# Mamba's first chunk: diagonals on GpSimd, both images' norms ahead of it, four PSUM buffers for its step sizes, the first state's products on VectorE

## The chip, the cores and the metric

The kernel runs on one core of a Trainium2 chip. The metric is the device time of one execution in microseconds (us). The core has five engines with a queue each: TensorE (PE in the profile), VectorE (DVE), ScalarE (ACT), GpSimd (POOL), and SyncE (SP), which here only issues DMAs. A queue is worked off in its order; an instruction that waits holds back all that stand behind it.

## The reference

The network has four layers on an input of 2 images, 256 channels and 32x32 positions. Only layer 0 is touched by the change. Cut to what it computes:

```python
x = x + layer0(group_norm(x))                 # groups of 8 channels, per image
# layer0: two Mamba blocks, the second on flipped channels
xs, res = split(u @ in_w + in_b)              # u: tokens x 256; xs, res: tokens x 512
xs = silu(causal_conv(xs, conv_w, 4 taps) + conv_b)
dt, B, C = split(xs @ xproj_w)                # 16, 16 and 16 columns
delta = softplus(dt @ dt_w + dt_b)            # the step sizes, tokens x 512
h[t] = exp(delta[t] * A) * h[t-1] + delta[t] * B[t] * xs[t]    # 16 states a channel
y[t] = sum over states of h[t] * C[t] + xs[t] * D
out = (y * silu(res)) @ out_w + out_b
u = u + layernorm(out)
```

Layers 1 to 3 (a 7x7 attention by convolution, linear attention with a mixture of experts, softmax attention with another) follow layer 0 and are the same in both kernels.

## The kernel before

All 2048 tokens of both images lie in `x`, channels on the partitions: two chunks of 128 channels by 1024 positions for each image. A Mamba block is worked off in four chunks of 512 tokens, the first two of image 0 and the last two of image 1; with two blocks there are eight units (`units` in `layer0`). A unit has three parts.

- `front` computes the inputs of the scan for one chunk: the projection `m_in` (L300) to `pre`, the convolution over four positions, `xd` (the small projection, L342) and its transposed third `ct`, then the step sizes: four matmuls `m_dt` (L370), one for each 128 of the 512 channels, and from each, softplus by |z|, Exp, Ln and corrections. `e` is the Exp, `ln` the logarithm, `delta` the step size, `du` the step size times `xs`. The very first `front` runs `alone=True`, ahead of any scan: its softplus and products are VectorE's and go by single channel blocks `dc`, and two of its four channel blocks are convolved by VectorE (L314, L319); the other two, like all of the later chunks, by TensorE with diagonal matrices (`taps`, L327).
- `scan` runs over 16 states `n`. For each, GpSimd forms two products `h = du * b` of 128x1024 (L450), where `b` is a row of B spread by DMA over the partitions; ScalarE forms the decay `da` in PSUM (L457); VectorE runs four scans of 512 tokens (L461). TensorE transposes the result into a PSUM bank `ht` (L429) and VectorE adds it, weighted by C, to `ya` (L438); for states 0 and 10 ScalarE writes it (L436). There are six buffers for `h`, that is three states.
- `back` applies the gate, the skip term (by the diagonal `skip` on TensorE, L496), the output projection and the layer norm.

Unit by unit, the scan of one unit, the front of the next and the back of the last are emitted interleaved: `paced` gives out steps of the others in 63 slots, one for each scan instruction. `load` fetches a block's weights and makes `taps`, 16 diagonals of 128x128, each the identity times a column of weights (L257); `load_rest` fetches the gate and output weights and makes the four `skip` diagonals (L277). For block 2 these are emitted in the steps of unit 3 and in those of unit 4.

This emitted order is a priority and not yet the queues' order. A planner goes over the whole program with estimated durations and gives each engine, when it takes it to be free, the first instruction in emitted order that it takes to be ready; buffers of a pool are handed out at the same time. So instructions can stand far ahead of their place in the source: the diagonals of block 2 ran at 348 to 367 us, in the third unit.

`GroupNorm.image(b)` normalises an image: `bn_stats` (L207) and `bn_aggr` (L208) for each channel's mean and variance, a matmul with a block matrix for the mean over the group (`gn_ps`, L210), the deviation (L215 to L217), a second matmul (L219), the square root on ScalarE (L146), and the normalisation in place (L225), four instructions of 128x512 for each image.

PSUM in this layer has eight banks: two for `mm` (all matmuls of front and back), three for `ht` (the transposes of the scan), three for `da`.

Of the kernel before, what the change touches and what calls it, by code (L numbers as in the profile page):

```python
# [19 lines left out]
P = 128  # L20
# [7 lines left out]
TC = 512  # L28
# [152 lines left out]
class GroupNorm:  # L181
# [18 lines left out]
    def image(self, b):  # L200
# [3 lines left out]
        for cc in range(NCC):  # L204
# [3 lines left out]
            nc.vector.bn_aggr(out=mv[:, cc, :], in_=st.rearrange("p h s -> p (h s)"))  # L208
        ps = self.psum.tile([P, TC], F32, tag="mm", name=f"gn_ps{b}")
        nc.tensor.matmul(ps[:, :n], lhsT=self.grp, rhs=mv[:, :, 0], start=True, stop=True)  # L210
# [6 lines left out]
        nc.vector.tensor_add(d, d, mv[:, :, 1])  # L217
        ps = self.psum.tile([P, TC], F32, tag="mm", name=f"gn_ps2{b}")
        nc.tensor.matmul(ps[:, :n], lhsT=self.grp, rhs=d, start=True, stop=True)  # L219
# [10 lines left out]
class Mamba:  # L230
# [14 lines left out]
    def load(self):  # L245
        net, nc, m, wpool = self.net, self.net.nc, self.m, self.wpool
        in_w, out_w, xproj_w, dt_w = self.weights
        self.in_sb = wpool.tile([P, NCC, DI], F32, tag="in_w", name=f"{m}_in_sb")
        nc.sync.dma_start(self.in_sb, in_w[:, :, :DI])
        self.xp_sb = wpool.tile([P, NDC, XD], F32, tag="xproj_w", name=f"{m}_xp_sb")  # L250
        nc.sync.dma_start(self.xp_sb, xproj_w)
        self.dt_sb = wpool.tile([RANK, DI], F32, tag="dt_w", name=f"{m}_dt_sb")
        nc.sync.dma_start(self.dt_sb, dt_w)

        self.taps = wpool.tile([P, NDC * 4, P], F32, tag="taps", name=f"{m}_taps")
        for i in range(NDC * 4):
            nc.vector.tensor_scalar_mul(  # L257
                self.taps[:, i, :], net.ident, net.col(f"{m}_conv_w", i)
            )
        self.aneg = wpool.tile([P, NDC * NS], F32, tag="aneg", name=f"{m}_aneg", bufs=2)  # L260
        nc.scalar.activation(self.aneg, net.col(f"{m}_A_log", 0, NDC * NS), AF.Exp)
        nc.vector.tensor_scalar_mul(self.aneg, self.aneg, -1.0)
        self.state = wpool.tile([P, NS, NDC], F32, tag="state", name=f"{m}_state", bufs=2)

    def load_rest(self):
# [10 lines left out]
        for dc in range(NDC):  # L276
            nc.vector.tensor_scalar_mul(self.skip[:, dc, :], net.ident, net.col(f"{m}_D", dc))  # L277
        yield
# [5 lines left out]
    def front(self, j, alone=False):  # L284
# [83 lines left out]
        for dc in range(NDC):  # L368
            ps = self.ps_mm.tile([P, TC], F32, tag="mm", name=f"{m}_dt_{j}_{dc}")
            nc.tensor.matmul(  # L370
# [33 lines left out]

    def scan(self, j, before, between):

# [37 lines left out]
        for n in range(NS):  # L444
# [3 lines left out]
            for g in range(NDC // G):  # L448
                h = scanp.tile(half, F32, tag="h", name=f"{m}_h_{j}_{n}_{g}", bufs=6)
                nc.gpsimd.tensor_mul(  # L450
                    h, du[:, g * G : (g + 1) * G, :], b.unsqueeze(1).to_broadcast(half)
# [112 lines left out]
def layer0(net, x, x_dram, m1, m2, load_image, taps, conv_dram, lg):  # L564
# [5 lines left out]
    with (  # L570
# [14 lines left out]
        ]  # L585
        norm = GroupNorm(net, wpool, ps_mm, x)
        blocks[0].load()
        load_image()
        for _ in blocks[0].load_rest():
# [4 lines left out]
        norm.image(0)  # L594
        units = [(m, j) for m in blocks for j in range(NCH)]
        for _ in units[0][0].front(0, alone=True):
            pass
        norm.image(1)
        before, done = iter(()), []
        aside = taps.make(ps_mm, conv_dram)  # L600
        for u, (m, j) in enumerate(units):
            steps = [(b, Mamba.GATED, 0, 35) for b in done]
            fronts = []
            for a, k in units[u + 1 : u + 2]:
                if k == 0:
                    a.load()
                fronts.append(a.front(k))
            rest = m.load_rest() if u and j == 0 else iter(())
# [7 lines left out]
            else:  # L616
# [17 lines left out]
                steps += [(taps.convolve(0, pair, acc), 56, 3, 63)]  # L634
            before = m.scan(j, before, paced(63, steps))
            done = [m.back(j)]
# [1059 lines left out]
```

## Time and profile before

| | us |
|---|---|
| three runs: lowest, median, highest | 2225.58, 2238.22, 2242.52 |
| the profiled execution | 2231.08 |
| its span, first to last instruction | 2229.4 |
| first scan instruction starts (L461) | 56.7 |
| last scan instruction starts | 1045.8 |

| engine | busy us | share of the span | instructions |
|---|---|---|---|
| TensorE, matmuls | 1917.7 | 86% | 8072 |
| VectorE | 1413.0 | 63% | 2180 |
| ScalarE | 1009.8 | 45% | 1686 |
| GpSimd | 1006.7 | 45% | 688 |

The shares are means over stages with different limits. The Mamba layer takes from the start to about 1046 us, the other layers the rest. The mean granted clock of TensorE was 0.91 of full speed.

In a timeline, each line gives start and duration in us, the engine, the source line, the operation, the tile written, an arrow, the tiles read, shapes, and how many instructions were merged; in brackets stands the time that the engine had been idle and what ended it. The duration of a merged line is from its first start to its last end.

### The profile page before, as it was taken

The numbers are of one execution on the slowest core, as the hardware profiler recorded it, in microseconds if no ns is written. First come the engines' busy times: TensorE is split into PE (matmuls) and PEld (weight loads), VectorE is DVE, ScalarE is ACT, GpSimd is POOL, SyncE is SP. The second block draws the span as 40 slices with busy tenths as digits, with TensorE's granted clock in tenths as the row PEclk, the third lists the DMA queues.
The fourth block names the chain that finished last, engine by engine and source line by source line (L and its number), as shares of the span: only waits on it lengthen the run. The fifth ranks groups of instructions, "written<-read, shape, count | busy, mean of one in ns | idle before, by whom it ended". The sixth has DMA issues, their size and how long they took to land.

```text
span 2229.4 us, 24288 instructions
## 1 busy us (share of the span) xinstructions
PE 1917.7 (86%) x8072; PEld 1207.2 (54%) x8072; DVE 1413.0 (63%) x2180; ACT 1009.8 (45%) x1686; POOL 1006.7 (45%) x688
## 2 busy tenths in 40 slices
PE   4789888897989889788999899859999699769995
PEld 1455555655555555454656556536665367546663
DVE  5999999999999999898104565642222533532223
ACT  4586766767777767644113544312221232212121
POOL 1687684968688786964025410013332000033330
PEclk8869988798989989799999999969999799879997
DMA  2111120211212111310030100038987200079996
GB/s 104 38 60 47 39 66 28 62 34 48 61 47 59 38 48 34 84 42 15 18 49 1 48 15 10 19 146 309 309 311 264 80 10 10 19 249 314 316 310 257
DMA packets 90022, 223.94 MB, mean 100 GB/s; under 512 B 35003, under 2 KB 51264, under 8 KB 79268
## 3 DMA queue, kind: packets, MB, share of 16 engines
q1 hardware_dynamic: 81620, 202.77, 27.5%
q0 software_dynamic: 7728, 19.15, 3.0%
q8 instruction: 67, 1.10, 0.2%
q10 hardware_dynamic: 544, 0.40, 0.1%
q14 instruction: 63, 0.52, 0.1%
HBM read 204.88 MB, written 19.37 MB: 101 GB/s over the span
## 4 chain that ended last, share of the span: by engine, by line
PE 32%; DVE 22%; issue 20%; POOL 13%; ACT 8%; DMA 4%; POOLq 0%; SPq 0%; DVEq 0%; ACTq 0%
DVE m_h L461 11%; DVE m_ya L438 6%; POOL x L1465 3%; PE acc L746 3%; POOL l_yd L1524 3%; POOL m_h L450 3%; PE m_ht L429 3%; PE early_acc L746 3%; PE av L1248 3%; DMA l_yd<-y,target 2%; PE sc L1222 2%; PE h L1083 2%; ACT m_da L457 2%; PE m_xd_ps L342 2%; PE w L1092 1%
## 5 line engine op out<-in xcount | busy, mean ns | idle before, releaser
L450 POOL TENSOR_TENSOR m_h<-m_du,m_b 128x1024 f32<-128x1024 f32 x256 | 602.2, 2375 | 241.0 <-PE m_ht L429 95.1
L429 PE MATMUL m_ht<-ident,m_h 128*128 128x128 f32 x2048 | 365.7, 308 | 135.8 <-DVE m_ya L438 83.8
L457 ACT ACTIVATE m_da<-m_delta,m_aneg 128x512 f32<-128x512 f32 x512 | 349.2, 690 | 224.1 <-DVE m_h L461 223.3
L429 PEld LDWEIGHTS m_ht<-ident,m_h 128*128 128x128 f32 x2048 | 265.1, 156 | 328.5 <-DVE m_ya L438 112.4
L1465 POOL DMA_INDIRECT x<-l_zd,source x82 | 83.5, 1018 | 599.9 <-DMA we<-in_l_experts_dram 223.5
L438 DVE SCALAR_TENSOR_TENSOR m_ya<-m_ht,m_ct,m_ya 128x512 f32<-128x512 f32 x448 | 318.7, 731 | 21.2 <-PE m_ht L429 20.9
L461 DVE TENSOR_TENSOR_SCAN m_h<-m_da,m_state,m_h 128x512 f32<-128x512 f32 x256 | 318.3, 1268 | 13.2 <-POOL m_h L450 8.0
L461 DVE TENSOR_TENSOR_SCAN m_h<-m_da,m_h 128x512 f32<-128x512 f32 x256 | 302.8, 1208 | 14.7 <-ACT m_da L457 11.5
L1493 PE MATMUL h<-we,xts 128*128 128x512 f32 x632 | 289.8, 602 | 2.5 <-DVE xts L1483 2.5
L1500 DVE TENSOR_TENSOR hid<-hid,h 128x512 f32<-128x512 f32 x79 | 54.3, 688 | 285.7 <-PE h L1493 281.8
L1493 PEld LDWEIGHTS h<-we,xts 128*128 128x128 f32 x632 | 115.8, 193 | 119.9 <-issue 116.4
L1511 ACT COPY hts<-ht 128x512 f32<-128x512 f32 x79 | 46.3, 586 | 276.6 <-PE ht L1507 276.6
L1518 PE MATMUL o<-we,hts 128*128 128x256 f32 x632 | 149.8, 380 | 2.2 <-DVE y L1523 1.5
L1524 POOL DMA_INDIRECT l_yd<-y,target x79 | 80.2, 1015 | 139.8 <-DVE y L1523 135.0
L1518 PEld LDWEIGHTS o<-we,hts 128*128 128x128 f32 x632 | 114.1, 190 | 16.6 <-issue 3.4
L327 PE MATMUL m_conv<-m_pre,m_taps 128*128 128x512 f32 x240 | 115.1, 603 | 6.5 <-ACT m_gate L487 5.6
L746 PE MATMUL early_acc<-x,early 128*98 128x448 f32 (+21 forms) x308 | 97.4, 448 | 0.0
L746 PE MATMUL acc<-x,pair 128*98 128x416 f32 (+21 forms) x308 | 94.2, 454 | 0.0
L1499 ACT ACTIVATE hid<-h 128x512 f32<-128x512 f32 x79 | 47.2, 597 | 87.9 <-PE h L1493 87.9
L1523 DVE COPY y<-o 128x256 f32<-128x256 f32 x79 | 33.6, 425 | 73.2 <-PE o L1518 73.2
L483 PE MATMUL m_g<-x,m_gate_sb 128*128 128x512 f32 x128 | 68.0, 641 | 2.1 <-ACT m_gate L487 1.3
L746 PEld LDWEIGHTS acc<-x,pair 128*98 128x98 f32 x308 | 47.9, 168 | 40.3 <-issue 34.8
(320 smaller groups left out, 2985.1 us busy)
## 6 DMA issues: line engine op xcount, KB each, us to landing
we<-in_l_experts_dram SPq DMA_DIRECT2D x82, 1536.0 KB
m_b<-m_bd SPq DMA_DIRECT2D x128, 256.0 KB
l_yl<-l_yd SPq DMA_DIRECT2D x16, 512.0 KB
w<-in_l_w_dram SPq DMA_DIRECT2D x21, 256.0 KB
l_zd<-l_z SPq DMA_DIRECT2D x8, 512.0 KB
early<-taps SPq DMA_DIRECT2D x7, 343.0 KB
pair<-taps SPq DMA_DIRECT2D x7, 343.0 KB
taps<-taps_sb SPq DMA_DIRECT2D x21, 98.0 KB
```

What stands on the lines that cost most here:

```text
L327: nc.tensor.matmul(ps, lhsT=self.taps[:, dc * 4 + k, :], rhs=pre[:, dc, k : k + TC], start=(k == 0), stop=(k == 3),)
L429: nc.tensor.transpose(ps[:, dc * P : (dc + 1) * P], hs[dc // G][:, dc % G, i * P : (i + 1) * P], net.ident,)
L438: nc.vector.scalar_tensor_tensor(ya[:, i, :], ps, c, ya[:, i, :], ALU.mult, ALU.add)
L450: nc.gpsimd.tensor_mul(h, du[:, g * G : (g + 1) * G, :], b.unsqueeze(1).to_broadcast(half))
L457: nc.scalar.activation(da, delta[:, dc, :], AF.Exp, scale=self.aneg[:, i : i + 1])
L461: nc.vector.tensor_tensor_scan(h, da, h, 0.0 if first else state[:, n, dc : dc + 1], ALU.mult, ALU.add)
L483: nc.tensor.matmul(ps, lhsT=self.gate_sb[:, kc, dc * P : (dc + 1) * P], rhs=xt[:, kc, tok], start=(kc == 0), stop=(kc == NCC - 1),)
L746: nc.tensor.matmul(a[:, lo - 16 * k : hi - 16 * k, co : co + n], lhsT=lhsT, rhs=self.x[:, kc, b, lo - r0 : hi - r0, ci : ci + n], start=(u ...
L1465: nc.gpsimd.indirect_dma_start(out=x, out_offset=None, in_=zd[:, :], in_offset=bass.IndirectOffsetOnAxis(ap=source[:, g : g + 1], axis=0), ...
L1493: nc.tensor.matmul(ps, lhsT=xt[:, kc * P : (kc + 1) * P], rhs=w12[:, s, kc, :], start=(kc == 0), stop=(kc == NCC - 1),)
L1518: nc.tensor.matmul(ps[:, :C], lhsT=ht[:, mc * P : (mc + 1) * P], rhs=w[:, 8 + mc, :], start=(mc == 0), stop=(mc == NHC - 1),)
L1524: nc.gpsimd.indirect_dma_start(out=yd[g], out_offset=bass.IndirectOffsetOnAxis(ap=target[:, g : g + 1], axis=0), in_=y, in_offset=None, bo ...
```

## The change

Four things change in layer 0.

- The 16 diagonals `taps` and the four `skip` of both blocks are made by GpSimd. The 16 are now a generator, `diagonals`: for block 1 it is run through after `load`, for block 2 it is handed out over the first eight slots of unit 3's steps.
- `norm.image(1)` is emitted right behind `norm.image(0)`, ahead of the first front, and both take their PSUM banks from the pool of the transposes, `ht`.
- In the first front (`alone`), the step-size matmuls of channel blocks 1 to 3 take their banks from `ht`, too, so that with one of `mm` four are in use.
- In the first unit, the products of state 0 are formed by VectorE.

```diff
@@ GroupNorm.image
-        ps = self.psum.tile([P, TC], F32, tag="mm", name=f"gn_ps{b}")
+        ps = self.psum.tile([P, TC], F32, tag="ht", name=f"gn_ps{b}")
...
-        ps = self.psum.tile([P, TC], F32, tag="mm", name=f"gn_ps2{b}")
+        ps = self.psum.tile([P, TC], F32, tag="ht", name=f"gn_ps2{b}")
@@ Mamba.load
         self.taps = wpool.tile([P, NDC * 4, P], F32, tag="taps", name=f"{m}_taps")
-        for i in range(NDC * 4):
-            nc.vector.tensor_scalar_mul(
-                self.taps[:, i, :], net.ident, net.col(f"{m}_conv_w", i)
-            )
...
+    def diagonals(self):
+
+        for i in range(NDC * 4):
+            self.net.nc.gpsimd.tensor_scalar_mul(
+                self.taps[:, i, :], self.net.ident, self.net.col(f"{self.m}_conv_w", i)
+            )
+            yield
@@ Mamba.load_rest
         for dc in range(NDC):
-            nc.vector.tensor_scalar_mul(self.skip[:, dc, :], net.ident, net.col(f"{m}_D", dc))
+            nc.gpsimd.tensor_scalar_mul(self.skip[:, dc, :], net.ident, net.col(f"{m}_D", dc))
@@ Mamba.front
-            ps = self.ps_mm.tile([P, TC], F32, tag="mm", name=f"{m}_dt_{j}_{dc}")
+            pool, tag = (self.ps_ht, "ht") if alone and dc else (self.ps_mm, "mm")
+            ps = pool.tile([P, TC], F32, tag=tag, name=f"{m}_dt_{j}_{dc}")
@@ Mamba.scan
-    def scan(self, j, before, between):
+    def scan(self, j, before, between, start=False):
...
-                nc.gpsimd.tensor_mul(
+                (nc.vector if start and n == 0 else nc.gpsimd).tensor_mul(
                     h, du[:, g * G : (g + 1) * G, :], b.unsqueeze(1).to_broadcast(half)
                 )
@@ layer0
-        norm = GroupNorm(net, wpool, ps_mm, x)
+        norm = GroupNorm(net, wpool, ps_ht, x)
         blocks[0].load()
+        for _ in blocks[0].diagonals():
+            pass
         load_image()
...
         norm.image(0)
         units = [(m, j) for m in blocks for j in range(NCH)]
+        norm.image(1)
         for _ in units[0][0].front(0, alone=True):
             pass
-        norm.image(1)
...
                 if k == 0:
                     a.load()
+                    steps.append((a.diagonals(), NDC * 4, 0, 8))
...
-            before = m.scan(j, before, paced(63, steps))
+            before = m.scan(j, before, paced(63, steps), u == 0)
```

## The prediction

> **What bounds the kernel now.** I first read the page's rows of busy tenths, to see which engine is full when. Each digit is one fortieth of the span, 55.7 us.
>
> ```profile
> PE   4789888897989889788999899859999699769995
> DVE  5999999999999999898104565642222533532223
> ```
>
> From slice 2 to slice 19, the Mamba layer, VectorE (DVE) stands at 9. Next the windows of that layer, with the sum of each engine's busy time:
>
> ```profile
> core 0: us, PE busy (x) PEld busy (x) DVE busy (x) ACT busy (x) POOL busy (x), PEclk, DMA share, GB/s
> 57.00:1046.00 989.00, 841.06 (x3883) 537.36 (x3883) 938.46 (x1081) 684.49 (x1105) 757.87 (x397) 0.88 0.17 48
> ```
>
> VectorE is busy 938 of 989 us (95%), TensorE 85%, GpSimd (POOL) 77%, ScalarE 69%. So from the first scan to the end of the layer VectorE is the bound, and an instruction taken off it there shortens the run by nearly its length. What follows 1046 us starts when the layer ends and is not touched. Ahead of 57 us no engine is full: there a chain decides. Its start, in the timeline of VectorE (start us, duration us, engine, line, operation; in brackets the idle time before):
>
> ```profile
> 8.31 3.19 DVE L257 TENSOR_SCALAR m_taps<-ident,cols_sb 128x128 f32<-128x128 f32 x16
> 11.42 0.87 DVE L277 TENSOR_SCALAR m_skip<-ident,cols_sb 128x128 f32<-128x128 f32 x4
> 12.20 0.15 DVE L212 COPY gn_gm<-gn_ps 128x2 f32<-128x2 f32 x1
> 15.52 1.91 DVE L225 TENSOR_SCALAR x<-x,gn_gm,gn_rs 128x512 f32<-128x512 f32 x4
> 22.80 0.55 DVE L314 TENSOR_SCALAR m_xs<-m_pre,cols_sb 128x512 f32<-128x512 f32 x1 [5.37 <-ACT m_pre L304]
> ```
>
> Image 0's group means are out of TensorE at 9.1 us (two L210 matmuls, 8.54 to 9.10), but VectorE builds 20 diagonals until 12.20 before it copies them. The first projection (L300) starts at 16.12, on the normalised image. VectorE is idle 5.37 us before 22.80. Then the step sizes, in the timelines of TensorE and ScalarE:
>
> ```profile
> 39.70 1.12 PE L370 MATMUL m_dt<-m_xd,m_dt_sb 16*128 16x512 f32 x2 [0.77 <-DVE m_delta L377]
> 42.71 2.07 PE L370 MATMUL m_dt<-m_xd,m_dt_sb 16*128 16x512 f32 x2 [1.89 <-DVE m_delta L377]
> 38.88 1.28 ACT L383 ACT_TABLE_LOAD   x1
> 43.02 1.28 ACT L386 ACT_TABLE_LOAD   x1
> 46.85 1.28 ACT L383 ACT_TABLE_LOAD   x1
> 48.79 1.28 ACT L386 ACT_TABLE_LOAD   x1
> ```
>
> With two PSUM buffers the third and fourth step-size matmuls wait for VectorE to empty a bank, so ScalarE goes Exp, Ln, Exp, Ln, with four table loads where two would do. The first scans, on VectorE:
>
> ```profile
> 54.01 2.71 DVE L399 TENSOR_TENSOR m_delta<-m_delta,m_ln 128x512 f32<-128x512 f32 x1
> 56.71 1.21 DVE L461 TENSOR_TENSOR_SCAN m_h<-m_da,m_h 128x512 f32<-128x512 f32 x1
> 59.63 1.31 DVE L217 TENSOR_TENSOR gn_d<-gn_d,gn_mv 128x2 f32<-128x2 f32 x1
> 64.58 8.73 DVE L225 TENSOR_SCALAR x<-x,gn_gm,gn_rs 128x512 f32<-128x512 f32 x4
> 73.23 4.55 DVE L461 TENSOR_TENSOR_SCAN m_h<-m_da,m_h 128x512 f32<-128x512 f32 x4
> ```
>
> Image 1's normalisation lies between the scans, at 2.2 us an instruction where image 0's took 0.54, while GpSimd runs seven products (L450) end to end. Last, the second Mamba block's diagonals, also in VectorE's queue:
>
> ```profile
> 348.13 4.95 DVE L257 TENSOR_SCALAR m_taps<-ident,cols_sb 128x128 f32<-128x128 f32 x8
> 361.98 0.46 DVE L257 TENSOR_SCALAR m_taps<-ident,cols_sb 128x128 f32<-128x128 f32 x2
> 363.61 3.43 DVE L257 TENSOR_SCALAR m_taps<-ident,cols_sb 128x128 f32<-128x128 f32 x6
> 629.64 2.78 DVE L277 TENSOR_SCALAR m_skip<-ident,cols_sb 128x128 f32<-128x128 f32 x3
> ```
>
> **What the Trainium skill says.** "SBUF — State Buffer", section "SBUF: two separate sides": VectorE and GpSimd share one pair of SBUF ports under an exclusive lock, which a VectorE instruction needs if it has two SBUF inputs or runs in a 2-port mode. The trace agrees: L225 0.54 against 2.24 us, L399 0.68 against 2.71, each beside L450 on GpSimd (2.36 us); the scan, with one input in PSUM, stays at 1.21. "ScalarE activation tables", section "What a function is on this engine": a switch of set is one load of 1283 ns; here 1.28.
>
> **The change, part by part.** Durations are of the profiled execution, 2231.1 us with a span of 2229.4.
>
> *Diagonals of block 1 to GpSimd.* Takes 3.19 + 0.78 us from VectorE ahead of 12.20. The copy of the means can then start at 9.2. From there to the first L225 took 3.3 us before (12.20 to 15.52), with image 1's statistics between the small steps; I keep that, since by the bytes moved image 1 lands at about 9.3 and 10.5 us. L225 at 12.5, L300 at 13.1: **-3.0 us** (-1.5 if a statistic stands in the queue before its data are there, -4 if none stands between). GpSimd is idle from 2.3 us on. A tensor_scalar on it is not in the trace. Nearest rows: affine_select on 128x128, 0.28 to 0.40 us; the product, 2.36 us for 1024 elements of two inputs. "GPSIMD Engine Reference", section "Elementwise — side-by-side cycle accounting", puts short bodies at 1.03 cycles an element. So 0.2 to 0.5 us, I take 0.35: begun with the columns at 5.5, the sixteen end at 11.1 and the skip's four at 12.5; the first conv matmul comes at 22.3 (25.3 - 3). Cost nothing. GpSimd's next work is the carry copy at 23, so nothing else queues behind them.
>
> *Image 1's normalisation before the first chunk.* Its 4 x 0.48 us of L225 and some 1 us of small steps fall behind image 0's, 14.4 to about 18, into the idle before L314 (19.8 after the shift): nothing, with 1.8 us of margin; without that cover it costs up to 3 us. TensorE gets four tiny matmuls (0.59 us a pair) and ScalarE one square root earlier, ahead of the first pre-activation at 17. Out of the scan stage go L225's 8.7, L217's 1.3, 0.6 of small steps, and on ScalarE two table loads.
>
> *Four buffers for the step sizes.* Count from the end of m_xd (36.53 before, 33.5 after). Before, the first Ln ended 8.5 us later; now four Abs go first (1.65 + 4 x 0.61 = 4.1), load (5.4), four Exp (7.75), load (9.05), Ln at 9.75: the first Ln is 1.3 us *later*. But by then VectorE has done all that hangs on Abs and Exp (4 x 0.70 + 4 x 0.95 = 6.6 us). The three banks from the transposes' pool are empty at about 8 us, long before the first transposes: nothing.
>
> *First state's products on VectorE.* Two tensor_mul of 128x1024, not in the trace on VectorE; 0.69 us for 512 elements and 0.53 of it streaming give 1.14 a piece back to back: +2.3. They spare the 5.46 us wait for GpSimd's first product, which VectorE's own tensor_tensors kept from the port (50.72 to 56.18).
>
> *Sum for the first chunk*, VectorE from the first Ln to the end of the fifth scan: 12 x 0.605 (softplus and du) + 2.3 + 5 x 1.13 + 0.5 left over + one port block of 2.1 (as L399's) = 17.8, so at 9.75 + 17.8 = 27.6 after m_xd. Before, that scan ended at 64.4 and VectorE was free for the next at 73.2, 36.7 after m_xd. Gain **-9.1** (-11.2 with no block, -5 with three). Next is VectorE again: GpSimd needs 4.7 us a state for two products, VectorE 7 to 8.
>
> *Block 2's diagonals.* VectorE loses 4.86 + 0.37 + 3.35 us of L257 and 2.71 + 0.71 of L277: 12.0 us (intervals to the next start). TensorE waited 5.4 us at 354.39 for VectorE, so they are on the path; I take **-10.5**, and -7 to -12 as bounds. GpSimd gets 20 x 0.35 = 7 us in a stage where it idles 12.6 us at 351.8 to 364.5 and three products lie ready ahead of the scans: nothing. The diagonals issue no DMA.
>
> Total -22.6: 2231.1 becomes 2208.5. The median, 2238.2, lies 7 us above the profiled run, and the four known runs (2225.6, 2231.1, 2238.2, 2242.5) have a mean of 2234.4. Taken from that mean: **2212 us**.
>
> **Rivals.** (a) *The port lock.* GpSimd starts the second state's products as soon as du is half done and alternates with VectorE's remaining tensor_tensors at 2.2 us each, as it did with L225. For: exactly that at 64.58. Against: VectorE's five back-to-back tensor_tensors at 51.48 to 53.89 kept GpSimd out. With five blocks the first chunk gains nothing: 2234.4 - 13.5 = 2221. (b) *VectorE's freed time becomes waiting* for TensorE, at 85% and a granted clock of 0.88: half of the second block's and the scan stage's gain lost, 2234.4 - 12 = 2222. For: TensorE's share. Against: the 5.4 us it waited. (c) *Nothing*: the order in the queues is planned over the whole layer, and another order gives the gain back: 2234. (d) *Slower: a GpSimd tensor_scalar costs d, far over 0.35 us.* Place: the conv diagonals of the first chunk (the twelfth, for its third channel block, is needed at 25.7, begun at 5.5: late by 12d - 20.2) and block 2's sixteen ahead of products (three states ahead, 23 us: late by 16d - 23). Price 28d - 43.2; it eats 22.6 at d = 2.35, and from d = 3.2 the run is slower by 1%, 2257. Against: affine_select at 0.28 to 0.40.
>
> **How the numbers follow.** Forecast 0.60, (a) 0.17, (b) 0.11, (c) 0.07, (d) 0.05. The forecast's own bounds are the sums of the ends, -13.5 to -27.2, and the runs of before spread by 8 us either way. One per cent, about what a measurement of this kernel can tell from no change, is 22.4 us: 2215.8. The forecast lies below it about 8 times in 10, (a) and (b) 2 in 10: 0.54 faster, 0.39 within, 0.07 slower. Range: 2198 (-27 and 9 for the runs) to 2229, which takes in (a) and (b).
>
> **What would show it.** Right: L212 near 9.3 us, L300 near 13; one Exp and one Ln load between Abs and the scans; no L225 after 20 us and all near 0.5; first scan near 49 to 51, the sixth near 61; L257 and L277 on GpSimd near 0.35 us; no such row on VectorE after 60. Wrong: tensor_tensors of 2 us or more on VectorE after the first du; diagonals over 1.7 us (12d = 20.2); more idle on VectorE between 80 and 1000 us, ended by TensorE or GpSimd.

## The result, and the profile after

| | before | after |
|---|---|---|
| median (range) of 4 executions, us | 2234.53 (2225.58 to 2242.52) | 2210.97 (2210.15 to 2212.91) |
| profiled execution, its span | 2231.08, 2229.4 | 2212.91, 2211.0 |
| first scan instruction ends | 57.9 | 55.0 |
| 16th (after four of the 16 states) | 91.6 | 78.6 |
| 64th (end of the first unit) | 178.4 | 164.7 |
| 192nd (end of the third unit) | 432.2 | 416.6 |
| 512th, the last | 1047.1 | 1031.8 |

After over before is 0.9897, 95% interval 0.9855 to 0.9938: faster by 1.0%. The forecast was 2212 us.

The lines of layer 0 moved down by three to six (before to after): L257 to L263 (taps), L277 to L280 (skip), L300 to L303 (`m_in`), L370 to L374 (`m_dt`), L377 to L381, L383 to L387 (Exp), L386 to L390 (Ln), L391 to L395, L395 to L399, L397 to L401, L399 to L403, L401 to L405 (du), L429 to L434 (transposes into `ht`), L438 to L443, L450 to L455 (products), L457 to L462 (decay), L461 to L466 (scan).

The rows of busy tenths, and the window from the first scan to the end of the layer, after:

```profile
PE   6888898897978888789999899859999699769995
DVE  6999998999999999897114666542222533532223
```

```profile
core 0: us, PE busy (x) PEld busy (x) DVE busy (x) ACT busy (x) POOL busy (x), PEclk, DMA share, GB/s
57.00:1028.00 971.00, 829.10 (x3859) 527.56 (x3858) 912.98 (x1050) 676.72 (x1096) 763.94 (x415) 0.89 0.17 49
```

The window stops 3.8 us short of the last scan's end, that of before only 1.1 us. Taken to that end in both, VectorE has 22.8 us less to do (939.56 to 916.78) in a stretch that is 15.3 us shorter; it is still the fullest engine, 94% against 95%. Where it happened, in VectorE's timeline after, from the start to the third unit:

```profile
8.65 0.16 DVE L212 COPY gn_gm<-gn_ps 128x2 f32<-128x2 f32 x1 [0.74 <-PE gn_ps L210]
...
10.90 1.29 DVE L207 BATCH_NORM_STATS2 gn_st<-x 128x6 f32<-128x512 f32 x2 [1.40 <-DMA x<-in_x_dram]
...
12.35 2.02 DVE L225 TENSOR_SCALAR x<-x,gn_gm,gn_rs 128x512 f32<-128x512 f32 x4
...
21.59 1.91 DVE L225 TENSOR_SCALAR x<-x,gn_gm,gn_rs 128x512 f32<-128x512 f32 x4
...
52.07 1.22 DVE L455 TENSOR_TENSOR m_h<-m_du,m_b 128x1024 f32<-128x1024 f32 x1
53.20 0.68 DVE L405 TENSOR_TENSOR m_du<-m_delta,m_xs 128x512 f32<-128x512 f32 x1
53.80 1.22 DVE L466 TENSOR_TENSOR_SCAN m_h<-m_da,m_h 128x512 f32<-128x512 f32 x1
54.94 2.40 DVE L455 TENSOR_TENSOR m_h<-m_du,m_b 128x1024 f32<-128x1024 f32 x1
57.26 7.90 DVE L466 TENSOR_TENSOR_SCAN m_h<-m_da,m_h 128x512 f32<-128x512 f32 x7
...
344.91 2.34 DVE L466 TENSOR_TENSOR_SCAN m_h<-m_da,m_h 128x512 f32<-128x512 f32 x2 [4.83 <-POOL m_h L455]
```

The means are copied at 8.65 instead of 12.20. Then VectorE waits 1.40 us for image 1's data with image 0's normalisation behind it in its queue. Image 1's normalisation now takes 1.91 us at 21.59, not 8.73 us between scans. One product (2.40 against 1.22) stood against GpSimd's products at the port. The last line is new: at 344.91 VectorE waits 4.83 us for a product of GpSimd's. The step sizes, on TensorE and on ScalarE:

```profile
34.69 3.69 PE L374 MATMUL m_dt<-m_xd,m_dt_sb 16*128 16x512 f32 x8
```

```profile
36.61 1.28 ACT L387 ACT_TABLE_LOAD   x1
...
41.84 1.28 ACT L390 ACT_TABLE_LOAD   x1
45.71 1.28 ACT L462 ACT_TABLE_LOAD   x1
```

The four matmuls (the profile lists two records for each) run without a pause; there is one load for Exp and one for Ln; the third, at 45.71, is the decay's. Last, GpSimd's timeline after, with the diagonals:

```profile
5.21 0.61 POOL L263 TENSOR_SCALAR m_taps<-ident,cols_sb 128x128 f32<-128x128 f32 x1 [3.37 <-DMA cols_sb<-in_cols_dram]
...
6.18 9.49 POOL L263 TENSOR_SCALAR m_taps<-ident,cols_sb 128x128 f32<-128x128 f32 x15
15.65 2.33 POOL L280 TENSOR_SCALAR m_skip<-ident,cols_sb 128x128 f32<-128x128 f32 x4
...
53.90 19.53 POOL L455 TENSOR_TENSOR m_h<-m_du,m_b 128x1024 f32<-128x1024 f32 x8
...
333.26 9.29 POOL L263 TENSOR_SCALAR m_taps<-ident,cols_sb 128x128 f32<-128x128 f32 x16
342.51 4.67 POOL L455 TENSOR_TENSOR m_h<-m_du,m_b 128x1024 f32<-128x1024 f32 x2
```

A diagonal takes 9.29 / 16 = 0.58 us on GpSimd, and block 2's sixteen stand in one piece ahead of products.

So the gain came early: -13.7 us by the end of the first unit, and only 1.6 us more from there to the last scan (-15.3), where the prediction had 10.5. The span is shorter by 18.3; the last 3 us lie behind the layer (1182.3 to 1179.2 us), in code that is the same. Of the other profiled kernels below, all with that code, none took over 1180.4 there, so that the 1182.3 belongs to this one execution of before and those 3 us are not the change's. From the 16th scan to the last, VectorE waited 48.5 us before (20.3 of it for TensorE, 11.1 for GpSimd) and 57.5 after (18.8 and 18.9). What the experiments had to find is where block 2's 10.5 us went.

### The profile page after: what moved, and what is told of

The parts are those of the page before. It is cut to its first block, busy times and chain, and to the rows that moved or that the text cites. A ratio compares the mean times of both kernels' runs of the same rounds, so it can differ in the third digit from the quotient of the medians.

```text
span 2211.0 us, 24284 instructions
## 1 busy us (share of the span) xinstructions
PE 1915.3 (87%) x8072; PEld 1201.8 (54%) x8072; DVE 1391.4 (63%) x2142; ACT 1003.4 (45%) x1682; POOL 1026.0 (46%) x726
## 3 DMA queue, kind: packets, MB, share of 16 engines
q1 hardware_dynamic: 81620, 202.77, 27.6%
## 4 chain that ended last, share of the span: by engine, by line
PE 32%; DVE 22%; issue 20%; POOL 11%; ACT 10%; DMA 4%; POOLq 0%; SPq 0%; DVEq 0%; ACTq 0%
DVE m_h L466 11%; DVE m_ya L443 6%; POOL x L1473 3%; PE acc L754 3%; POOL l_yd L1532 3%; PE m_ht L434 3%; PE early_acc L754 3%; PE av L1256 3%; ACT m_da L462 2%; DMA l_yd<-y,target 2%; PE sc L1230 2%; PE h L1091 2%; POOL m_h L455 2%; PE m_xd_ps L345 1%; PE w L1100 1%
## 5 line engine op out<-in xcount | busy, mean ns | idle before, releaser
L455 POOL TENSOR_TENSOR m_h<-m_du,m_b 128x1024 f32<-128x1024 f32 x254 | 594.3, 2365 | 196.3 <-PE m_ht L434 96.1
L434 PE MATMUL m_ht<-ident,m_h 128*128 128x128 f32 x2048 | 362.8, 306 | 117.7 <-DVE m_ya L443 81.9
L462 ACT ACTIVATE m_da<-m_delta,m_aneg 128x512 f32<-128x512 f32 x512 | 349.4, 690 | 220.4 <-DVE m_h L466 219.8
L434 PEld LDWEIGHTS m_ht<-ident,m_h 128*128 128x128 f32 x2048 | 260.5, 155 | 316.3 <-DVE m_ya L443 111.3
L443 DVE SCALAR_TENSOR_TENSOR m_ya<-m_ht,m_ct,m_ya 128x512 f32<-128x512 f32 x448 | 320.2, 733 | 18.8 <-PE m_ht L434 17.2
L466 DVE TENSOR_TENSOR_SCAN m_h<-m_da,m_state,m_h 128x512 f32<-128x512 f32 x256 | 318.5, 1270 | 13.5 <-POOL m_h L455 8.5
L466 DVE TENSOR_TENSOR_SCAN m_h<-m_da,m_h 128x512 f32<-128x512 f32 x256 | 303.1, 1209 | 23.6 <-ACT m_da L462 13.2
L303 PE MATMUL m_in<-x,m_in_sb 128*128 128x512 f32 x128 | 68.8, 663 | 10.2 <-ACT m_pre L307 6.9
```

The costliest lines, as they stand in the source:

```text
L303: nc.tensor.matmul(ps, lhsT=self.in_sb[:, kc, mc * P : (mc + 1) * P], rhs=self.xt[:, kc, tok], start=(kc == 0), stop=(kc == NCC - 1),)
L434: nc.tensor.transpose(ps[:, dc * P : (dc + 1) * P], hs[dc // G][:, dc % G, i * P : (i + 1) * P], net.ident,)
L443: nc.vector.scalar_tensor_tensor(ya[:, i, :], ps, c, ya[:, i, :], ALU.mult, ALU.add)
L455: (nc.vector if start and n == 0 else nc.gpsimd).tensor_mul(h, du[:, g * G : (g + 1) * G, :], b.unsqueeze(1).to_broadcast(half))
L462: nc.scalar.activation(da, delta[:, dc, :], AF.Exp, scale=self.aneg[:, i : i + 1])
L466: nc.vector.tensor_tensor_scan(h, da, h, 0.0 if first else state[:, n, dc : dc + 1], ALU.mult, ALU.add)
```

## Experiments

Two readings of the missing gain stood against each other. **The lump:** VectorE's time is worth its length, and it was lost because GpSimd's sixteen diagonals, at 0.58 us and in one piece, hold back a product that VectorE then waits for. **Waiting for TensorE**, the prediction's rival (b): VectorE's freed time is mostly not to be had, whatever GpSimd does. The single parts were then run alone and left out, for the prediction's other steps.

Times and ratios are against runs of the kernel before on the same chip; "64th" and "192nd" are the ends of those scan instructions in the profiled execution.

| kernel | median us | ratio [95%] | 16th | 64th | 192nd | last scan |
|---|---|---|---|---|---|---|
| after, once more | 2212.59 | 0.9898 [0.9864, 0.9932] | 79.2 | 166.2 | 418.4 | 1031.2 |
| block 2's diagonals on VectorE | 2216.43 | 0.9919 [0.9888, 0.9950] | 77.3 | 164.1 | 419.5 | 1035.3 |
| taps in four tiles | 2206.81 | 0.9884 [0.9852, 0.9915] | 78.5 | 164.6 | 412.6 | 1022.8 |
| block 2's taps twice | 2222.34 | 0.9947 [0.9931, 0.9962] | 77.4 | 163.4 | 424.6 | 1040.1 |
| only block 1's diagonals | 2232.42 | 0.9987 [0.9971, 1.0003] | 88.5 | 178.6 | 436.4 | 1051.9 |
| only the norms | 2224.97 | 0.9951 [0.9934, 0.9969] | 83.0 | 168.7 | 424.0 | 1040.6 |
| only the buffers | 2243.72 | 1.0025 [1.0004, 1.0045] | 95.3 | 184.5 | 439.6 | 1066.5 |
| only the products | 2229.72 | 0.9961 [0.9935, 0.9988] | 87.1 | 173.7 | 429.0 | 1056.0 |
| after, products by GpSimd | 2212.67 | 0.9884 [0.9854, 0.9913] | 78.9 | 166.9 | 418.0 | 1030.0 |
| after, two buffers | 2213.44 | 0.9889 [0.9861, 0.9917] | 78.7 | 165.9 | 420.9 | 1031.7 |
| four tiles, image 1 loaded later | 2205.49 | 0.9849 [0.9827, 0.9872] | 76.4 | 162.3 | 409.7 | 1024.3 |

### The changed kernel once more

No edit; it shows how far two profiled executions of one kernel lie apart.

> The changed kernel once more, unaltered, as the measure of repetition. If the queues' orders decide layer 0, its last scan ends within 0.5 us of the 1031.8 us of the first profile and the time lies within 2 us of 2211; if the granted clock moves it, both may move by 5 us or more.

Measured: 2212.59 us; the 16th scan ends 0.6 us later than in the first profile, the 192nd 1.8 later, the last 0.6 earlier. Single points inside the layer are thus good to about 2 us.

### Block 2's diagonals back on VectorE

```diff
@@ Mamba.diagonals
-            self.net.nc.gpsimd.tensor_scalar_mul(
+            (self.net.nc.gpsimd if self.m == "m1" else self.net.nc.vector).tensor_scalar_mul(
@@ Mamba.load_rest
-            nc.gpsimd.tensor_scalar_mul(self.skip[:, dc, :], net.ident, net.col(f"{m}_D", dc))
+            (nc.gpsimd if m == "m1" else nc.vector).tensor_scalar_mul(...)
@@ layer0
-                    steps.append((a.diagonals(), NDC * 4, 0, 8))
+                    for _ in a.diagonals():
+                        pass
```

> The changed kernel with block 2's 20 diagonals back on VectorE. Theory 1 (on GpSimd the sixteen taps stand in one lump of 9.3 us ahead of the next products, and VectorE then waits 4.8 us for a product, so the move gave only some 2.3 us net): the last scan ends 2 to 4 us later than in the changed kernel, near 1034 to 1036 us. The prediction's step (the move is worth 10.5 us): near 1042 us. Theory 2 (VectorE's freed time turns into waiting for TensorE anyway, so the move is worth nothing): 1031 to 1033 us, and with a lump gone no wait of VectorE for a product near 340 us but waits for TensorE.

Measured: 2216.43 us against 2212.59 for the changed kernel in the same series, 3.8 more; the last scan ends at 1035.3 against 1031.2 and 1031.8. VectorE's timeline in this kernel has them again:

```profile
336.36 4.93 DVE L263 TENSOR_SCALAR m_taps<-ident,cols_sb 128x128 f32<-128x128 f32 x8
350.19 0.46 DVE L263 TENSOR_SCALAR m_taps<-ident,cols_sb 128x128 f32<-128x128 f32 x2
351.82 3.43 DVE L263 TENSOR_SCALAR m_taps<-ident,cols_sb 128x128 f32<-128x128 f32 x6
```

and GpSimd's timeline around them:

```profile
335.38 4.65 POOL L455 TENSOR_TENSOR m_h<-m_du,m_b 128x1024 f32<-128x1024 f32 x2 [3.16 <-ACT m_xs L336]
352.67 4.81 POOL L455 TENSOR_TENSOR m_h<-m_du,m_b 128x1024 f32<-128x1024 f32 x2 [12.64 <-issue]
```

What follows: the move is worth some 4 us where 10.5 were predicted. The second fence says where the cover lay. GpSimd's 12.64 us of idling, which the prediction took as the place for the diagonals, lie from 340.0 to 352.7, behind the pair of products that starts at 335.38. Ahead of that pair GpSimd idled 3.16 us only, and that is where the changed kernel has its lump (at 333.26, with the pair following at 342.51). The 12.64 us are also in part VectorE's own doing: it spends 8.8 us on diagonals between 336.36 and 355.25 and uses up products later (the next experiment shows how much of the idling is left without them). This kernel alone does not part the two readings: a product that is late and a TensorE that is late would both leave 4 us.

### The taps in four tiles, one for each channel block

```diff
-        self.taps = wpool.tile([P, NDC * 4, P], F32, tag="taps", name=f"{m}_taps")
+        self.taps = [
+            wpool.tile([P, 4, P], F32, tag=f"taps{dc}", name=f"{m}_taps{dc}") for dc in range(NDC)
+        ]
...
-                self.taps[:, i, :], self.net.ident, self.net.col(f"{self.m}_conv_w", i)
+                self.taps[i // 4][:, i % 4, :], self.net.ident, self.net.col(f"{self.m}_conv_w", i)
...
-                    ps, lhsT=self.taps[:, dc * 4 + k, :], rhs=pre[:, dc, k : k + TC],
+                    ps, lhsT=self.taps[dc][:, k, :], rhs=pre[:, dc, k : k + TC],
```

With one tile, no diagonal of block 2 can be written until block 1's last convolution has read all sixteen; with four, each group follows its own channel block. The same instructions on the same engine.

> The changed kernel with the taps in four tiles, one for each channel block, so that GpSimd's sixteen diagonals of block 2 come in lumps of 3, 4, 5 and 4 between products as each block of convolutions is done with its tile. Theory 1: the 4.8 us wait of VectorE for a product near 340 us goes, and the last scan ends 4 to 5 us earlier, near 1027 us. Theory 2: it ends within 1.5 us of 1031.8, and the idle time of VectorE in that unit (10.8 us) stays and is ended by TensorE or ScalarE.

Measured: 2206.81 us, 5.8 below the changed kernel and 9.6 below the kernel with these diagonals on VectorE, in the same series. GpSimd's timeline:

```profile
312.80 1.76 POOL L265 TENSOR_SCALAR m_taps<-ident,cols_sb 128x128 f32<-128x128 f32 x3 [3.38 <-PE m_conv L332]
314.52 4.67 POOL L457 TENSOR_TENSOR m_h<-m_du,m_b 128x1024 f32<-128x1024 f32 x2
319.17 0.60 POOL L265 TENSOR_SCALAR m_taps<-ident,cols_sb 128x128 f32<-128x128 f32 x1
320.63 1.76 POOL L265 TENSOR_SCALAR m_taps<-ident,cols_sb 128x128 f32<-128x128 f32 x3 [0.86 <-PE m_conv L332]
322.36 4.68 POOL L457 TENSOR_TENSOR m_h<-m_du,m_b 128x1024 f32<-128x1024 f32 x2
327.02 2.92 POOL L265 TENSOR_SCALAR m_taps<-ident,cols_sb 128x128 f32<-128x128 f32 x5
329.90 4.67 POOL L457 TENSOR_TENSOR m_h<-m_du,m_b 128x1024 f32<-128x1024 f32 x2
334.56 2.34 POOL L265 TENSOR_SCALAR m_taps<-ident,cols_sb 128x128 f32<-128x128 f32 x4
...
348.09 2.36 POOL L457 TENSOR_TENSOR m_h<-m_du,m_b 128x1024 f32<-128x1024 f32 x1 [6.02 <-issue]
```

And VectorE's waits between 280 and 430 us (releaser; us in total, times, longest), first in the changed kernel and then in this one:

```profile
DVE m_h L466 <- POOL m_h L455: 7.8, 4, 4.8
DVE m_h L466 <- ACT m_da L462: 4.9, 7, 1.3
DVE m_ya L443 <- PE m_ht L434: 0.8, 2, 0.4
```

```profile
DVE m_h L468 <- ACT m_da L464: 4.1, 6, 1.3
DVE m_h L468 <- POOL m_h L457: 2.8, 4, 1.3
DVE m_ya L445 <- PE m_ht L436: 2.3, 5, 1.1
```

What follows: lumps of three to five, with a state's products between, instead of one of sixteen; the waits for GpSimd fall from 7.8 to 2.8 us and the longest from 4.8 to 1.3. Waiting for TensorE rises by 1.5, far less than the gain. The lump is the cause; rival (b) would have left this kernel where the changed one is. The last line shows that of the 12.64 us of idling at this place 6.02 remain with the diagonals off VectorE: about half of the cover that the prediction counted on was there, but one pair of products behind the lump. The last scan ends 9.0 us earlier than in the changed kernel, where 4 to 5 were expected; 5.0 of it are the shorter waits for GpSimd, the rest is not traced.

### Block 2's taps formed twice

```diff
-            self.net.nc.gpsimd.tensor_scalar_mul(
-                self.taps[:, i, :], self.net.ident, self.net.col(f"{self.m}_conv_w", i)
-            )
+            for _ in range(1 if self.m == "m1" else 2):
+                self.net.nc.gpsimd.tensor_scalar_mul(
+                    self.taps[:, i, :], self.net.ident, self.net.col(f"{self.m}_conv_w", i)
+                )
```

> The changed kernel with each of block 2's sixteen taps formed twice on GpSimd, in the same place in the queue (one lump of 18.6 us in place of 9.3). Theory 1: VectorE's wait of 4.8 us grows by the 9.3 us, to 14 us, and the last scan ends 7 to 9 us later, near 1040 us. Theory 2: the lump is hidden by the products ready ahead and the last scan ends within 2 us of 1031.8.

Measured: 2222.34 us, 9.8 above the changed kernel. GpSimd's and VectorE's timelines:

```profile
329.21 18.64 POOL L264 TENSOR_SCALAR m_taps<-ident,cols_sb 128x128 f32<-128x128 f32 x32
```

```profile
350.19 2.34 DVE L467 TENSOR_TENSOR_SCAN m_h<-m_da,m_h 128x512 f32<-128x512 f32 x2 [14.17 <-POOL m_h L456]
```

What follows: the lump grew by 18.64 - 9.29 = 9.35 us, VectorE's wait by 14.17 - 4.83 = 9.34. Once the lump is longer than what lies ready, every microsecond of it is on the path. The slack ahead of the changed kernel's lump was therefore some 9.29 - 4.83 = 4.5 us, not the 23 of the prediction. All four profiles with the sixteen in one lump have the wait: 4.8 to 5.1 us.

The other profiles agree with this when all are sorted by where block 2's diagonals are made. From the 64th scan to the 192nd (units two and three, with the taps) and from the 192nd to the last (with the skip's diagonals), means and ranges in us:

| block 2's diagonals | kernels | 64th to 192nd | 192nd to last |
|---|---|---|---|
| on VectorE | before; block 2's on VectorE; only block 1's diagonals; only the norms | 255.6 (253.8 to 257.8) | 615.7 (614.9 to 616.6) |
| GpSimd, one tile | after, twice; products by GpSimd; two buffers | 252.5 (251.1 to 255.0) | 612.7 (610.8 to 615.2) |
| GpSimd, four tiles | four tiles; image 1 later | 247.7 (247.4 to 248.0) | 612.4 (610.2 to 614.6) |
| GpSimd, formed twice | taps twice | 261.2 | 615.5 |

The kernels with only the buffers and only the products, diagonals on VectorE too, have 255.1 and 255.3 in the first column but 626.9 and 627.0 in the second; between 660 and 1000 us their granted clock was 0.87, where the eleven others had 0.89 to 0.92; the order of instructions on the four engines is there the one of the kernel with only the norms. They are left out of the second mean and, to keep the rows alike, of the first. The sixteen taps gave 255.6 - 252.5 = 3.1 of their 8.6 us in one lump, and 7.9 in four. The skip's four gave at most 615.7 - 612.7 = 3.0 of their 3.4 us. This 3.0 is not shown to be theirs: single profiles spread by as much (taps twice, with them on GpSimd, has 615.5), and the granted clock differs too (0.89 to 0.91 in the first row, 0.91 to 0.92 in the second).

### Only block 1's diagonals

The kernel before, with `taps` and `skip` of block 1 made by GpSimd:

```diff
-            nc.vector.tensor_scalar_mul(
+            (nc.gpsimd if m == "m1" else nc.vector).tensor_scalar_mul(
                 self.taps[:, i, :], net.ident, net.col(f"{m}_conv_w", i)
...
-            nc.vector.tensor_scalar_mul(self.skip[:, dc, :], net.ident, net.col(f"{m}_D", dc))
+            (nc.gpsimd if m == "m1" else nc.vector).tensor_scalar_mul(...)
```

> The kernel before with block 1's 20 diagonals alone on GpSimd. Compared is the end of the 16th scan instruction (the fourth state of the first unit): 91.6 us before, 78.6 us with the whole change. By the prediction's sum for this part, 3.0 us less, or 2.3 us by what the changed kernel showed at its m_xd: 88.5 to 89.5 us. If the start is not on the path: 91.6.

Measured: the first step size's instruction on VectorE starts at 35.86 us against 38.90, -3.0, and the 16th scan ends 3.0 earlier. By the end of the first unit that is gone (178.6 against 178.4), and in time the kernel is the one before: 0.9987 [0.9971, 1.0003]. What follows: the -3.0 of the start is right at its place. From the 16th scan to the 64th VectorE waited 6.6 us where it was 3.8 before, 5.1 of it against 3.3 for TensorE's transposes; why these came later was not tried.

### Only the norms

The kernel before, with `norm.image(1)` ahead of the first front and both norms' banks from `ht`:

```diff
-        norm = GroupNorm(net, wpool, ps_mm, x)
+        norm = GroupNorm(net, wpool, ps_ht, x)
...
+        norm.image(1)
         for _ in units[0][0].front(0, alone=True):
             pass
-        norm.image(1)
```

> The kernel before with image 1's normalisation alone moved ahead of the first front (both on the transposes' banks). By the prediction, VectorE loses 8.7 + 1.3 + 0.6 us between the scans and ScalarE two table loads, and image 1's small steps fill VectorE's idle time ahead of the convolution: the 16th scan ends 9 to 10 us earlier, at 81.5 to 83 us. If the port lock finds other victims (VectorE's last tensor_tensors beside GpSimd's products, 2.2 us each): 84 us or more.

Measured: the 16th scan ends 8.6 us earlier, and half a per cent of the time is gone (0.9951). It would be more, but in VectorE's timeline two waits show what the normalisation had covered:

```profile
56.67 1.22 DVE L461 TENSOR_TENSOR_SCAN m_h<-m_da,m_h 128x512 f32<-128x512 f32 x1 [2.24 <-POOL m_h L450]
...
62.66 6.96 DVE L461 TENSOR_TENSOR_SCAN m_h<-m_da,m_h 128x512 f32<-128x512 f32 x6 [2.46 <-POOL m_h L450]
```

GpSimd's first products are late, and VectorE waits 4.7 us for them. It is the largest single part of the change.

### Only the four buffers

The kernel before, with the one change in `front`:

```diff
-            ps = self.ps_mm.tile([P, TC], F32, tag="mm", name=f"{m}_dt_{j}_{dc}")
+            pool, tag = (self.ps_ht, "ht") if alone and dc else (self.ps_mm, "mm")
+            ps = pool.tile([P, TC], F32, tag=tag, name=f"{m}_dt_{j}_{dc}")
```

> The kernel before with four PSUM banks alone for the first chunk's step sizes. By the prediction the first Ln comes 1.3 us later and two table loads go, while VectorE has done its part ahead; VectorE then still meets GpSimd's first product and image 1's normalisation: the 16th scan ends within 2 us of 91.6 us, rather earlier. If the table loads are on the path at their full 2 x 1.28 us: 89 us.

Measured: slower, 1.0025 [1.0004, 1.0045], and the 16th scan 3.7 us later: a miss. VectorE's timeline:

```profile
44.10 0.16 DVE L212 COPY gn_gm<-gn_ps 128x2 f32<-128x2 f32 x1 [3.59 <-PE gn_ps L210]
...
47.89 0.69 DVE L398 TENSOR_TENSOR m_ln<-m_ln,m_du 128x512 f32<-128x512 f32 x1
```

What follows: in this kernel image 1's norm still comes behind the first front. The copy of its mean now stands in VectorE's queue ahead of the step sizes, and waits 3.59 us for a matmul of two columns; all of the softplus is queued behind it. A buffer changed the planned order, and the order cost more than the buffer was worth. The profile's last scan is 19.4 us later; 12.0 of it come behind the 192nd scan, in the stage with the low granted clock (see the table by groups), which the kernel with only the products shows as well.

### Only the products

The kernel before, with the first state's two products on VectorE (the edit of `scan` and the argument `u == 0`, as in the change).

> The kernel before with the first state's products alone on VectorE. By the prediction +2.3 us of VectorE against a first product that GpSimd got only after 3 us of waiting for the port: the 16th scan ends within 2 us of 91.6 us, rather earlier (first scan at 54 to 55 us in place of 56.7). If GpSimd's next products take the port from VectorE's own: later, 93 us or more.

Measured: the 16th scan ends 4.4 us earlier, more than expected, but not where expected. The first scan starts later, at 60.07 against 56.71; the gain is in the line of the normalisation:

```profile
60.07 1.21 DVE L461 TENSOR_TENSOR_SCAN m_h<-m_da,m_h 128x512 f32<-128x512 f32 x1
...
66.99 2.82 DVE L225 TENSOR_SCALAR x<-x,gn_gm,gn_rs 128x512 f32<-128x512 f32 x4
```

It takes 2.82 us where it took 8.73. GpSimd's products ended at 68.16 and it stood still until 71.60, so that only the start of the normalisation met one. What follows: the port is worth more than the two products, but this gain is the same as that of the norms moved away; the two do not add (beside the other parts the products are worth 1.4 us, as the next experiment shows).

The four parts alone sum to -3.0 - 8.6 + 3.7 - 4.4 = -12.3 us at the 16th scan; all together gave -13.0. Part of each figure is the start: with the same order in the queues, the first step size begins anywhere from 35.26 to 37.20 us. Counted from there to the 16th scan, before takes 52.7 us, only block 1's diagonals 52.7, only the norms 43.7, only the buffers 55.5, only the products 47.4, and all six profiles of kernels that have the four parts in the first chunk 42.0.

### The change without the products on VectorE

```diff
-            before = m.scan(j, before, paced(63, steps), u == 0)
+            before = m.scan(j, before, paced(63, steps))
```

> The changed kernel with the first state's products back on GpSimd. Compared is the end of the 16th scan instruction: 78.6 and 79.2 us in the two profiles of the changed kernel. If the part is worth with the others what it was alone (4.4 us): 83 us. By the prediction's own sum (+2.3 us of VectorE against a wait for the port of about 3): 79 to 80 us. If the block that VectorE's second product met (2.40 us in place of 1.2) outweighs it: 78 us or less.

Measured: 2212.67 us, the time of the changed kernel. Counted from the first step size on VectorE (35.46 here, 36.63 in the changed kernel; the wait for image 1's data was 0.56 us and not 1.40), the 16th scan ends after 43.4 us against 42.0. In VectorE's timeline GpSimd's first product slips in among the softplus and blocks one instruction (2.56 us; the same line at 37.40 took 0.43), and a later scan waits:

```profile
46.95 2.56 DVE L395 TENSOR_SCALAR m_du<-m_e 128x512 f32<-128x512 f32 x1
...
57.30 6.96 DVE L466 TENSOR_TENSOR_SCAN m_h<-m_da,m_h 128x512 f32<-128x512 f32 x6 [1.32 <-POOL m_h L455]
```

What follows: beside the other parts the products are worth 1.4 us, too little for the time to show.

### The change with two buffers

The last edit undone: `ps` from `mm` for all four channel blocks.

> The changed kernel with two PSUM banks for the first chunk's step sizes, as before. Theory 1 (the 3.7 us that four banks cost alone came from image 1's small steps, for which VectorE waited 3.59 us in that kernel, so that with the norms ahead the banks save the two table loads): the 16th scan ends later than 78.6 to 79.2 us, by 0.5 to 3 us. Theory 2 (four banks delay the first Ln, and that is on the path in any company): it ends earlier, at 75 to 77 us.

Measured: 2213.44 us, again the time of the changed kernel. From the first step size (35.27) to the 16th scan it takes 43.5 us against 42.0. ScalarE loads its tables five times up to the decay (35.26 to 47.74 us) instead of three. VectorE's timeline:

```profile
53.68 1.86 DVE L404 TENSOR_TENSOR m_du<-m_delta,m_xs 128x512 f32<-128x512 f32 x1
...
56.60 2.46 DVE L454 TENSOR_TENSOR m_h<-m_du,m_b 128x1024 f32<-128x1024 f32 x1
```

What follows: with the norms out of the way the buffers no longer cost and give 1.5 us. That is clear in this stretch, which is 41.98 to 42.00 us in the six profiles of kernels with all four parts there, and too little for the time to show. The two table loads are nearly hidden behind VectorE, which has softplus work for most of that time (it waits 1.61 us for the first Ln, 0.92 in the changed kernel): two blocks at the port (1.86 and 2.46) instead of one make up most of the 1.5.

### Four tiles, and image 1 loaded behind the gate and output weights

The kernel with four tiles, and:

```diff
-        load_image()
         for _ in blocks[0].load_rest():
             pass
+        load_image()
```

> The kernel with taps in four tiles, and image 1 loaded behind the gate and output weights, so that VectorE's queue has image 1's statistics behind image 0's normalisation. In the changed kernel VectorE waited 1.4 us for image 1's data with image 0's square root done at 10.4 us. If that wait is on the path, image 0's normalisation starts at 10.6 us in place of 12.4, the 16th scan ends near 77 us, and the time falls 1.5 to 2 us below that of the kernel with taps in four tiles (ratio 0.9884 to before): ratio 0.987 to 0.988. If image 1's normalisation, now later, collides with the convolution on VectorE: 78.5 us or more and no gain.

Measured: 2205.49 us, 0.9849 [0.9827, 0.9872], the shortest time of all; against the four tiles alone (2206.81, in another series) the difference is too small to tell. The 16th scan ends 2.1 us earlier than with four tiles alone. VectorE's timeline:

```profile
10.54 0.17 DVE L147 RECIPROCAL gn_rs<-gn_rs 128x2 f32<-128x2 f32 x1 [0.98 <-ACT gn_rs L146]
10.74 2.02 DVE L225 TENSOR_SCALAR x<-x,gn_gm,gn_rs 128x512 f32<-128x512 f32 x4
...
25.25 1.92 DVE L225 TENSOR_SCALAR x<-x,gn_gm,gn_rs 128x512 f32<-128x512 f32 x4
```

Image 0's normalisation starts at 10.74 us instead of 12.35, since no statistic of image 1 stands ahead of the reciprocal any more. Image 1's moved on from 21.59 to 25.25, still ahead of the scans, and costs ScalarE two more table loads (at 23.45 and 25.03). The first step size starts 36.63 - 34.41 = 2.2 us earlier than in the changed kernel, and ahead of all seven profiles that load image 1 first (35.26 to 37.20).

## Why the prediction was right, and where it was wrong

**The time.** 2212 us was forecast, 2210.97 measured; the most likely case came true. That it came within 1 us is luck. The sum behind it was -22.6 us; the one profile of before against the two of the changed kernel gives -18.3 (spans 2229.4 to 2211.0 and 2211.1), of which 3 lie behind the layer. The medians differ by 23.6 in one series and 20.0 in the next, because executions of before spread over some 17 us. So the total is within what can be told, but one of its three terms was much too large.

**The start, -3.0.** Right. In the changed kernel the projection starts at 12.96 us (16.12 before; near 13 was the sign), although VectorE's queue waited 1.40 us for image 1's data. Of these 3.2 us 2.3 were left at the first step size (36.63 against 38.90), but over the seven profiles with this start it comes at 35.26 to 37.20, 36.0 in the mean, which is 2.9 earlier. The wait at a statistic of image 1, which the prediction had named, was 0.56 to 1.71 us in these profiles; loading image 1 later took it away.

**The first chunk, -9.1.** The mechanism is right; that the figure is right to 0.1 us is in part luck. From the end of `m_xd` (34.26) the fifth scan ends after 27.6 us, as worked out, but the parts within differ. The first scan started at 53.80, not at 49 to 51, since the planner put softplus of later channel blocks ahead of it. The block at the port cost 2.40 - 1.22 = 1.2 us, not 2.1; about as much more of the left-over softplus came after the first Ln than the 0.5 allowed (two L399 and one L395, 1.5 us from start to start), and the two misses cancel. A product on VectorE took 1.13 us from start to start, against 1.14. Its own duration is 1.22, which agrees with an estimate by the formula of the Trainium skill, "VectorE: DVE Perf Modes", section on the TRN2 errata: (1024 + 151) cycles at 0.96 GHz.

**The norms at no cost.** Right: 1.91 us in the idle time before the convolution's later blocks, four instructions near 0.5 as said, though at 21.59 us and not by 20. **The buffers** were a step with no gain of their own in the sum; left out of the change they cost 1.5 us, alone they made the 16th scan 3.7 later, through an order that the prediction had not looked for.

**Block 2's diagonals, -10.5.** This step failed, in "in a stage where it idles 12.6 us ... and three products lie ready ahead of the scans: nothing". Measured are at most -6.1 (3.1 for the taps, up to 3.0 for the skip) from the profiles, and -3.8 in the timed pair. The sign of being wrong that it had named came: VectorE's waits for GpSimd grew by 7.8 us between the 16th scan and the last (4.8 in the second profile of the changed kernel). Three things were wrong in it.

- *The size.* 0.58 us a diagonal, not 0.35 and outside the bounds of 0.2 to 0.5. These were drawn from affine_select (0.28 to 0.40) and from the Trainium skill's "GPSIMD Engine Reference", section "Elementwise — side-by-side cycle accounting", whose 1.03 cycles an element count the body alone; the 128 elements of a row would be 0.11 us at the 1.2 GHz that the section computes with, so some 0.47 us of each instruction here are not the body. That is an estimate from the page; no run varied the size.
- *The place.* One tile for sixteen diagonals is released at once, so that they stand in one lump of 9.29 us. This is rival (d)'s place. Its price was 16d - 23, nothing up to d = 1.4 us. The runs give a lump's length less 4.5, at d = 0.58 already 4.8 us. Three states were not ready ahead: when the lump begins, the scans of all products but half of the last pair have started (154 scans, 78 products of two scans each). Before's trace has it too: at 348.13, where VectorE turns to the diagonals, 78 products were formed and all of their 156 scans had started.
- *The cover.* The 12.6 us of idling on GpSimd lie behind the pair of products that the lump holds up, so that they covered nothing of it; and about half of them came from the diagonals on VectorE (6.02 us remain with four tiles).

With four tiles the taps gave 7.9 of their 8.6 us, so the other half of the step, that VectorE's time counts by its length, holds.

**The rivals.** (a) The port lock with five blocks: no, one block of 1.2 us; VectorE's run of two-input instructions kept GpSimd out, as argued: a copy of 128x12 on GpSimd (L299) took 4.04 us from 49.90 to 53.94, where it had taken 0.65 before. (The run of before that was cited, 51.48 to 53.89, has four such instructions, not five.) (b) VectorE waiting for TensorE: refuted as the cause of block 2's loss. VectorE's waits for TensorE between the 16th scan and the last are 20.3 us before, 18.8 and 22.0 in the two profiles of the changed kernel. It is there in small: the second unit (64th to 128th scan) became 4.8 us longer in the changed kernel (122.2 to 127.0), and between 224 and 293 us VectorE waited 4.0 us for TensorE and not for GpSimd; TensorE's granted clock was 0.50 between 270 and 285 us. But with the products by GpSimd it was 0.50 there, too, and the unit took 122.3; in the kernel with image 1 loaded later it takes 122.6. What decides it was not settled; the table by groups takes in both units for this reason. (c) Nothing: no, although one part alone, block 1's diagonals, did just that.

## What to carry to other kernels

Before you hide work in an engine's idle time, ask what makes it idle, since part of the cover goes with the work that you move (12.64 us became 6.02), and whether the work will really stand in it. In this kernel the engine that feeds the bound one could take extra work without loss only in pieces shorter than its slack, 4.5 us here, and the size of a buffer decided the size of a piece: sixteen diagonals in one tile cost a wait of 4.8 us, in four tiles none longer than 1.3. And a statistic or a copy that waits, first in the queue of the bound engine, holds back all behind it, however small it is (1.40 us at the start; 3.59 us with the buffers alone).

## What the runs showed of the hardware

A multiplication of 128x128 by a column takes 0.58 us from start to start on GpSimd, and 0.20 alone on VectorE at the start (3.19 us for sixteen), though 0.57 to 0.62 beside GpSimd's products (3.43 us for six, 4.93 for eight): in that place VectorE was no faster.
